# Gated attention with a mixture of experts on one core: zero products at the start, the first x tiles on two queues, an earlier weight copy, and another form and order for a few score tiles

## The chip, the core and the metric

The kernel runs on one core of a Trainium2 chip. The core has a matmul engine (PE, with weight loads shown as PEld), a vector engine (DVE), a scalar engine (ACT), GpSimd (POOL) and SyncE (SP), each with an instruction stream of its own that runs in order, and 16 DMA engines that move data between the main memory and the core's own memory. DMAs are issued here by SP, ACT and POOL. The metric is the device time of one execution in microseconds.

## The reference

x has 2 batches of 2048 rows of 512 numbers. Cut to what matters:

```
xn  = layernorm(x)
a   = layernorm(xn) * gamma + beta           # the attention's own norm
q, k, v = a @ Wq, a @ Wk, a @ Wv
out = softmax(causal(q k^T / sqrt(512))) @ v @ Wo + xn
f   = sum over the 2 best of 8 experts of gate * (silu(xn @ W1[e] + b1[e]) @ W2[e] + b2[e])
y   = x + out * silu(f)
```

## The kernel before

**Stages.** All matmuls are in float32, and the trace shows two records for each of them. (1) Wq and Wk are folded into one 512 x 512 matrix `wqk`, and Wv and Wo into `wvo` (`fold`, L207). Each fold goes over four row blocks c of its two sources; for every block it needs that block of both. (2) Eight blocks of 512 rows are normalised (`norm`), transposed into keys, and multiplied with `wqk` and `wvo`; for five of them by seven half-size products in place of eight (`seven_products`, L400). (3) `route` picks two experts for each row and sorts the rows. (4) The experts work through 68 steps of 128 rows (`up` L882, `down` L921). In the last of them a tile holds 64 rows for each of two experts; the second expert's weights are copied into `w1c` by ACT and into `w2c` by DVE (`copy_w2`, L869). The PE runs the two 64-wide streams side by side. (5) Attention goes over 32 query tiles of 128 rows in the order `seq` (L811), as pairs.

**How the work is ordered.** The whole order is written by hand: under `tc.manual_schedule()` every engine gets its instructions in program order. A step `s` of the attention's loop issues the scores of tile `seq[s]`, the softmax of the same tile, and the product with v of an earlier tile. `widths[s]` are the chunks of 512 keys of a tile, the last one cut at the diagonal.

**The start.** `load_raw(c, (0, 1))` issues row block c of the first source on SP and of the second on ACT. After c = 1, `load(0)` issues the four tiles of the first x block, all on SP (L160). Then follow the rest of the row blocks, `load(1)`, eight small loads, and the sources of the second fold: `parts[2]` on SP, `parts[3]` (o_proj) on ACT. The second fold follows the transposes of block 0 (L286). `gw` is a tile that DVE sets to zero at the start (L165) and that gets the router's weights later.

**The end of the experts.** `experts_step(i)` (L934 and following) issues for step i: the copy of w2c for tile i - 3, the output copy of tile i - 4, the join of the transposed halves for tile i - 2, and `down` of tile i - 3. After the last full step, the scores of tile 0 of the attention (`chunk_scores`, L994, maxima L982) are issued, and then the last expert steps.

**Scores by seven products.** For a pair in `FAST` (L959), the first 1024 keys of both tiles are scored together by `fast_scores` (L1046): 7 products of two half-depth matmuls, and sums of them on DVE (L1052). It needs sums of the queries (`query_sums`, L1013 to L1016) and of the first two key blocks (`block_sums`, L1027). The first product is copied to the score tile by ACT (L1065). A pair outside `FAST` is scored tile by tile (`chunk_scores`) and its exponentials (L1138) read the matmul's result directly. `FAST` also sets whether the products with v of a pair go by seven products (`combine_p`, `combine_v` L1210, L1236) or straight (`values`, L1188).

**Softmax to values.** The exponentials go to POOL, which splits the 16-bit halves (L1148), by a transposing DMA (L1154) and to DVE, which joins the halves (`join_p`, L1170). Tiles with at most 384 keys are transposed by PE (`turn_p`, L1165). `gather_y` (L1333) fetches the experts' rows and `gate` (L1343 to L1346) scales them; `attended` (L1351, L1354) and `emit` finish a tile.

**The second batch.** Its pairs come in the order 8-9, 0-1, 6-7, 2-3, 4-5, 10-11, 12-13, 14-15; the last three are in `FAST`. The table `later` (L1401) names the steps at whose end DVE prepares differences of the second batch's v blocks and key blocks, one instruction at a time.

Of the kernel before, what the change touches and what calls it, by code (L numbers as in the profile page):

```python
# [10 lines left out]
F32 = mybir.dt.float32  # L11
# [9 lines left out]
P = 128  # L21
# [5 lines left out]
def gated_attention_moe(  # L27
# [27 lines left out]
    nc = tc.nc  # L55
    B, S, D = x.shape
    E, _, H = w1_t.shape
    KEY = o_proj.shape[0]
    NT = B * S // P
    BT = 4  # L60
    TB = BT * P
    NB = NT // BT
    NBB = S // TB
# [9 lines left out]
    NS = -(-((2 * NT * P + E * (HALF - 1)) // HALF) // 2)  # L73
# [83 lines left out]
    def load(b):  # L157
        xt = xp.tile([P, BT, D], F32, name=f"x_{b}", tag="x")
        for t in range(BT):
            nc.sync.dma_start(out=xt[:, t, :], in_=xb[:, b * BT + t, :])  # L160
        xin[b] = xt

    GW = P // ND
# [540 lines left out]
        put(LAST - 5 + e, load_w1, e)  # L704

    in_order = ctx.enter_context(tc.manual_schedule())
    for c in range(NK):
        load_raw(c, (0, 1))
        if c == 1:
            load(0)  # L710
# [97 lines left out]

    assert B == 2 and NBB == 4
    seq = [t for t in reversed(range(NBB * BT))]  # L810
    seq += [NBB * BT + t for t in (8, 9, 0, 1, 6, 7, 2, 3, 4, 5, 10, 11, 12, 13, 14, 15)]  # L811
    assert all(seq[s] // 2 == seq[s + 1] // 2 for s in range(0, NT, 2))
    fetch_k = fetch(aks, lambda: kp2, kt_d, "k2", "kT")
    fetch_v = fetch(avs, lambda: vp, v_d, "v2", "v")
# [5 lines left out]
    DOWN = 3  # L820
# [44 lines left out]
    def copy_w2(i):  # L865
        if i >= FULL:
            ev = expert(places(i)[1][1], mybir.EngineType.DVE)
            for rows, c in ((P, slice(0, NH - 1)), (HL + 1, slice(NH - 1, NH))):
                nc.vector.tensor_copy(  # L869
                    w2c[:rows, c, :],  # L870
                    w2[:rows, bass.ds(ev, 1), c, :].rearrange("p o c d -> p (o c) d"),
                )
# [61 lines left out]
    def experts_step(i):  # L934


        def at(f, k):
            if 0 <= i + k < NS:
                f(i + k)

        at(copy_w2, -DOWN)
        at(keep_y, -DOWN - 1)
        if i >= 0:
            at(gather, FIRST)
        at(turn, 3)
        at(join, 1)
        at(join_h, -2)
        at(up, 0)
        at(turn_h, 0)
        at(copy_w1, 1)  # L950
        at(down, -DOWN)
# [5 lines left out]


    FAST = (0, 1, 2, 3, 13, 14, 15)  # L959

    def place(s):
        b, t = divmod(seq[s], BT)
# [21 lines left out]

    def direct(s):

        return range(2 if s // 2 in FAST else 0, len(widths[s]))

    def chunk_scores(s, j):
        b, t, first = place(s)  # L990
# [16 lines left out]
    def query_sums(s, engine):  # L1007

        q = qsums[s] = sq.tile([P, 4, ND // 2, P], F32, name=f"sq_{s}", tag="sq")
        (a11, a12), (a21, a22) = (  # L1010
            [aqs[seq[s] // 2][:, d, ts(seq[s + i] % 2, P)] for d in kds] for i in range(2)
        )
        engine.tensor_tensor(q[:, 0], a21, a22, ALU.add)  # L1013
        engine.tensor_tensor(q[:, 1], q[:, 0], a11, ALU.subtract)
        engine.tensor_tensor(q[:, 2], a11, a21, ALU.subtract)
        engine.tensor_tensor(q[:, 3], a12, q[:, 1], ALU.subtract)  # L1016
# [90 lines left out]
    for i in range(NS):  # L1107
        experts_step(i)
        if i >= 8 and i % 2 == 0 and early:
            f, b, c = early.pop(0)  # L1110
            f(b, c)
            if not early:
                query_sums(0, nc.gpsimd)
    for s in range(2):
        begin_scores(s)
    for j in direct(0):
# [277 lines left out]
    K = NBB  # L1394
# [5 lines left out]

    later = {}  # L1401
    for steps, f, b in (
        ((10, 10, 11, 11), combine_v, K + 2), ((12, 12, 13, 13), combine_v, K + 1),
        ((20, 21, 22, 23), block_sums, K), ((24, 25, 26, 27), combine_v, K),
    ):
        for i, step in enumerate(steps):
            later.setdefault(step, []).append((f, b, (i + 1,)))
# [6 lines left out]

    for s in range(NT + OUT + 2):
        fast = s // 2 - 1 in FAST
        pair = (s, s + 1) if s // 2 in FAST else (s,)
        if s < NT and (s % 2 == 0 or len(pair) == 1):
            for k in pair:
                if s:  # L1420
                    begin_scores(k)
                room(k)
        n = s // 2 + 1
        if s % 2 == 0 and NQ <= n < NT // 2:
            for c in range(2):
                fetch_q(n, c)
        if s == 0:
            fetch_parts(s, NBB * ND)
            block_sums(0)
        late = []  # L1430
        for k in range(NT):
            if k not in AHEAD:
                wait = 4 - k % 2 if k // 2 in FAST else 3
                if s == k + wait:
                    late.append((attended, k))
                if s == k + wait + 1:
                    emit(k)
        if len(pair) == 1 or s % 2:
            for f, *args in late:
                f(*args)  # L1440
        for k in range(NT):
            if s == (NT - 1 if k in AHEAD else k + 2 - k % 2 if k // 2 in FAST else k + 1):
                fetch_inputs(k)
        if s == NT - 1:
            gather_y(NT - 2)
        if s % 2 and s > 3 and s // 2 + 1 in FAST:
            query_sums(s + 1, nc.vector)
        joins = []
        for k in () if s == 1 else (0, 1) if s == 2 else (s - 1,):
            if 0 <= k < NT - 1 and not by_te(k):  # L1450
                joins += [(join_p, k)] * len(halves[k])
        chunks = []
        if s < NT and s != 1:
            chunks = [(k, j) for k in ((1,) if s == 0 else (s,)) for j in direct(k)]
        if s == 0:

            for k, j in chunks:
                chunk_scores(k, j)
            chunks = []
        if s < NT and s % 2 == 0 and len(pair) == 2:  # L1460
            pools = [(ps_a, "a")] * 5 + [(ps_b, "b"), (ps_a, "a")]
            if s < 3:
                pools = [(ps_b, "b")] * 3 + [(ps_a, "a")]
            if s == 2:
                joins = [(combine_v, b, (1,)) for b in range(NBB - 1)] + joins
            now = 5 if s == 2 else 1
            fast_scores(s, pools, late + joins[:now])
            joins = joins[now:]
            if s == 0:
                query_sums(2, nc.gpsimd)  # L1470
        for k, j in chunks:
            chunk_scores(k, j)
            if s != 3 and joins:
                f, *args = joins.pop(0)
                f(*args)
        if s != 3:
            for f, *args in joins:
                f(*args)
        if 0 <= s - 1 < NT and by_te(s - 1):

            values(s - 2)
            turn_p(s - 1)
        if s < NT and s != 1:
            end_scores(s)
        if fast and s % 2 == 0 and 2 < s < NT:
            combine_p(s - 2)
        if 0 <= s - 1 < NT:
            divisor(s - 1)
        if s < NT:
            if s != 1:  # L1490
                exponentials(s)
            if s % 2 == 0 and len(pair) == 2:
                maximum(s + 1, turned[s + 1][:, : 2 * TB], 0)
            if s == 0:
                end_scores(1)
                exponentials(1)
            fetch_parts(s, 4)
            for f, *args in later.pop(s, []):
                f(*args)
        if s == 2:  # L1500
            pass
        elif s == 3:
            combine_p(0, (1, 3, 2))
            for b in range(NBB - 1):
                combine_v(b, (2,))
            values_first(0)
            combine_p(0, (4,))
            for b in range(NBB - 1):
                combine_v(b, (4,))
            values_next(0)  # L1510
            for f, *args in joins:
                f(*args)
            values_end(0, [lambda: query_sums(s + 1, nc.vector)])
        elif fast and s % 2 == 0:
            values_first(s - 2)

            if s != NT - 2:
                values_next(s - 2)
        elif fast and s == NT - 1:
            values_next(s - 3)  # L1520
            gate(s - 1)
            values_end(
                s - 3, [lambda: join_p(s)] * len(halves[s]) + [lambda: combine_p(s - 1)]
            )
            for k in AHEAD:
                make_ahead(k)
        elif fast:
            values_end(s - 3)
        elif 0 <= s - 2 < NT and not (s - 1 < NT and by_te(s - 1)):
            values(s - 2)  # L1530

        for k in range(0, NT - 2, 2):
            if s == (k + 2 if k + 2 in AHEAD else k + 3):
                gate(k)
        for k in range(0, NT - 2, 2):
            if s == k + 1:
                gather_y(k)
        if s == 1:
            for b in range(NBB - 1):
                combine_v(b, (3,), nc.gpsimd)  # L1540
    att.close()

# [43 lines left out]
```

## Time and profile before

| | us |
|---|---|
| median of 3 runs | 1054.38 (1052.28 to 1054.64) |
| the profiled execution | 1051.26 |
| its span on the core | 1049.5 |
| PE busy | 1036.8 (99%) |
| DVE busy | 633.6 (60%) |
| POOL busy | 435.1 (41%) |
| ACT busy | 332.2 (32%) |
| first matmul | 3.93 |
| start of the attention's first scores | 592.65 |
| start of the second batch's first scores | 819.45 |

How to read it: the span begins with the first instruction and ends with the last, and the execution's own time is a little longer. A row of the timeline has the start, the length, the engine, the line, the operation, out<-in by the program's names, the shape, the number of merged instructions and in brackets the idle time before and what ended it. A row of the waits has the engine and line that waited, what it waited for, and total us, times and the longest. A row of the chain has start, length, engine, name and line, and the number of records. The columns of the DMA view are equal slices of the window that was asked for (here 0 to 24 us, 40 slices of 0.6 us).

### The profile page before, as it was taken

The numbers are of one execution on the slowest core, as the hardware profiler recorded it, in microseconds if no ns is written. First come the engines' busy times: TensorE is split into PE (matmuls) and PEld (weight loads), VectorE is DVE, ScalarE is ACT, GpSimd is POOL, SyncE is SP. The second block draws the span as 40 slices with busy tenths as digits, with TensorE's granted clock in tenths as the row PEclk, the third lists the DMA queues.
The fourth block names the chain that finished last, engine by engine and source line by source line (L and its number), as shares of the span: only waits on it lengthen the run. The fifth ranks groups of instructions, "written<-read, shape, count | busy, mean of one in ns | idle before, by whom it ended". The sixth has DMA issues, their size and how long they took to land.

```text
span 1049.5 us, 12196 instructions
## 1 busy us (share of the span) xinstructions
PE 1036.8 (99%) x3554; PEld 616.1 (59%) x3554; DVE 633.6 (60%) x1195; ACT 332.2 (32%) x675; POOL 435.1 (41%) x469
## 2 busy tenths in 40 slices
PE   8999999999999999999999999999999999999998
PEld 3688886444555555555545445776765544447577
DVE  4798884775333333333335468796656556789686
ACT  3222311211332232232246313213334554532340
POOL 2364250003433333335332117444656777764272
PEclk9999999999999999999999999999999999999999
DMA  8699999946999999999887256534767868754361
GB/s 304 180 283 288 296 240 329 344 163 172 195 238 225 225 218 240 224 230 229 198 189 165 64 197 163 143 91 123 192 175 223 269 188 229 184 139 126 96 158 41
DMA packets 300513, 209.34 MB, mean 199 GB/s; under 512 B 234520, under 2 KB 247576, under 8 KB 299424
## 3 DMA queue, kind: packets, MB, share of 16 engines
q1 hardware_dynamic: 281248, 146.12, 56.7%
q0 software_dynamic: 10560, 35.17, 13.3%
q10 hardware_dynamic: 8640, 27.27, 7.1%
q8 instruction: 30, 0.49, 0.2%
q14 instruction: 35, 0.29, 0.1%
HBM read 92.89 MB, written 60.03 MB: 146 GB/s over the span
## 4 chain that ended last, share of the span: by engine, by line
PE 84%; DMA 5%; DVE 3%; issue 3%; POOL 2%; ACT 1%; SPq 1%; ACTq 0%; DVEq 0%; POOLq 0%
PE py L921 16%; PE ph L882 16%; PE ps L994 13%; PE p L1236 9%; PE p L1046 8%; PE po L1188 7%; PE p L400 7%; DMA w<-in_w_t_dram 2%; PE p L1188 2%; PE pj L341 2%; PE pw L207 2%; PE pj L346 1%; DMA zuT<-zu 1%; ACT w1c L863 1%; POOL xs L768 1%
## 5 line engine op out<-in xcount | busy, mean ns | idle before, releaser
L921 PE MATMUL py<-w,ht 128*128 (+3 forms) x408 | 187.1, 594 | 0.0
L882 PE MATMUL ph<-w,xT 128*128 (+1 forms) x544 | 173.1, 460 | 0.7 <-POOL keep L1103 0.7
L929 DVE COPY y<-py 128x512 f32<-128x512 f32 x68 | 46.9, 690 | 174.1 <-PE py L921 170.5
L907 ACT ACTIVATE ht<-ht,b1sel 128x128 f32<-128x128 f32 (+3 forms) x237 | 73.1, 375 | 224.0 <-DVE ht L901 224.0
L994 PE MATMUL ps<-k,q 128*128 128x512 f32 (+3 forms) x416 | 143.0, 495 | 0.0
L882 PEld LDWEIGHTS ph<-w,xT 128*128 128x128 f32 (+1 forms) x544 | 97.4, 181 | 73.4 <-issue 34.5
L892 POOL COPY hu<-h 128x704 uint16<-128x704 uint16 x68 | 52.7, 775 | 203.6 <-ACT h L890 114.1
L1148 POOL COPY pu<-pT 128x1024 uint16<-128x1024 uint16 (+2 forms) x74 | 82.0, 1139 | 116.7 <-issue 53.1
L921 PEld LDWEIGHTS py<-w,ht 128*128 128x128 f32 (+3 forms) x408 | 73.4, 182 | 75.5 <-issue 38.4
L994 PEld LDWEIGHTS ps<-k,q 128*128 128x128 f32 x416 | 74.6, 190 | 67.6 <-issue 58.6
L768 POOL DMA_INDIRECT xs<-zu_d,toki x68 | 69.0, 1014 | 70.1 <-DVE toki L642 58.8
L1333 POOL DMA_INDIRECT yg<-y_d,posi x64 | 68.2, 1065 | 38.3 <-DVE yg L1344 22.8
L1188 PE MATMUL po<-v,pT 128*128 128x512 f32 x182 | 81.0, 592 | 0.0
L264 POOL COPY zu<-z 128x1024 uint16<-128x1024 uint16 x32 | 35.2, 1099 | 78.2 <-DVE z L249 78.2
L1170 DVE COPY pT<-puT 128x1024 uint16<-128x1024 uint16 (+2 forms) x74 | 54.9, 772 | 7.4 <-DMA puT<-pu 4.7
L1188 PEld LDWEIGHTS po<-v,pT 128*128 128x128 f32 x182 | 34.2, 190 | 38.1 <-issue 36.4
L413 DVE TENSOR_TENSOR so<-p,so 128x512 f32<-128x512 f32 x70 | 45.8, 686 | 15.2 <-DMA v_d<-so 9.0
L842 DVE COPY xT<-xhT 128x1024 uint16<-128x1024 uint16 x68 | 47.1, 692 | 11.0 <-DMA xhT<-xs 6.0
L1138 ACT ACTIVATE pT<-pT,nm 128x1024 f32<-128x1024 f32 x14 | 16.1, 1149 | 110.3 <-DVE nm L1082 71.3
L1138 ACT ACTIVATE pT<-ps,nm 128x512 f32<-128x512 f32 (+3 forms) x52 | 30.0, 580 | 61.0 <-DVE nm L1082 38.9
L1354 DVE SCALAR_TENSOR_TENSOR o<-xo,xscale,o 128x512 f32<-128x512 f32 x30 | 28.8, 965 | 33.3 <-ACT o L1351 32.0
L1052 DVE TENSOR_TENSOR pT<-p,pT 128x512 f32<-128x512 f32 x49 | 32.9, 687 | 25.9 <-PE p L1046 18.7
(246 smaller groups left out, 1705.7 us busy)
## 6 DMA issues: line engine op xcount, KB each, us to landing
y_d<-y SPq DMA_DIRECT2D x68, 256.0 KB
zu_d<-zu SPq DMA_DIRECT2D x32, 264.0 KB
x<-in_x_dram SPq DMA_DIRECT2D x32, 256.0 KB
kt_d<-kT ACTq DMA_DIRECT2D x8, 1024.0 KB
k<-kt_d SPq DMA_DIRECT2D x32, 256.0 KB
q<-qt_d SPq DMA_DIRECT2D x32, 256.0 KB
v<-v_d SPq DMA_DIRECT2D x32, 256.0 KB
xo<-in_x_dram SPq DMA_DIRECT2D x32, 256.0 KB
```

The lines of the kernel that those rows point to most:

```text
L400: nc.tensor.matmul(ps[:, r, :], lhsT=lhs[:, c, ts(r, P)], rhs=rhs[:, c, :], start=(c == 0), stop=(c == 1),)
L768: nc.gpsimd.indirect_dma_start(out=xs, out_offset=None, in_=zu_d, in_offset=bass.IndirectOffsetOnAxis(ap=toki[:, i : i + 1], axis=0),)
L882: nc.tensor.matmul(ph[at, :], lhsT=xT[:, c, at], rhs=rhs[k], start=(c == 0), stop=(c == ND - 1),)
L907: nc.scalar.activation(ht[:hn, c, at], ht[:hn, c, at], AF.Silu, bias=b1sel[:hn, c, j : j + 1])
L921: nc.tensor.matmul(py[at, :], lhsT=ht[:k, c, at], rhs=rhs[n], start=(c == 0), stop=(c == NH - 1),)
L994: nc.tensor.matmul(ps[:, :w], lhsT=aqs[seq[s] // 2][:, c, ts(t % 2, P)], rhs=aks[first + j][:, c, :w], start=(c == 0), stop=(c == ND - 1),)
L1046: nc.tensor.matmul(ps, lhsT=x[:, c], rhs=y[:, c], start=(c == 0), stop=(c == ND // 2 - 1))
L1148: nc.gpsimd.tensor_copy(pu[:, : 2 * w].rearrange("p (h d) -> p h d", h=2), turned[s][:, k : k + w].bitcast(U16).rearrange("p (d h) -> p h ...
L1170: nc.vector.tensor_copy(turned[s][:, k : k + w].bitcast(U16).rearrange("p (i t h) -> p i t h", t=P, h=2), puT[:, : 2 * w // P, :].rearrang ...
L1188: nc.tensor.matmul(dst, lhsT=turned[s][:, ts(k, P)], rhs=avs[first + k // BT][:, k % BT, cols], start=(start and k == k0), stop=(k == k1 - 1),
L1236: nc.tensor.matmul(dst, lhsT=a[:, k], rhs=v(k), start=(k == 0), stop=(stop and k == n - 1))
L1333: nc.gpsimd.indirect_dma_start(out=y, out_offset=None, in_=y_d, in_offset=bass.IndirectOffsetOnAxis(ap=posi[k][:, n : n + 1], axis=0),)
```

## The change

It has six parts. (a) Six products of zeros (`gw` with itself, 128 x 128) are issued on PE ahead of everything else. (b) The second and fourth tile of the first x block are issued on ACT's queue, the others stay on SP's. (c) The copy of w2c for the first expert tile after the last full step is issued ahead of the attention's first scores; in `experts_step(NS)` it is left out. (d) The second batch's first pair (steps 16 and 17, tiles 8 and 9) is scored by `fast_scores`; its product with v stays as it was. Its key sums are prepared at the ends of steps 13 to 15, and v differences of block K + 1 move from steps 12 and 13 to 20 to 23. At step 17 the joins of tile 8's halves are issued behind the exponentials of tile 9. (e) The pair 6-7 comes ahead of the pair 0-1. (f) Three POOL instructions at step 1 are issued for the blocks 2, 0, 1 in place of 0, 1, 2.

```diff
     def load(b):
...
-            nc.sync.dma_start(out=xt[:, t, :], in_=xb[:, b * BT + t, :])
+            queue = nc.scalar if b == 0 and t % 2 else nc.sync
+            queue.dma_start(out=xt[:, t, :], in_=xb[:, b * BT + t, :])
...
     in_order = ctx.enter_context(tc.manual_schedule())
+    warm = ps_t.tile([P, TB], F32, name="warm", tag="pt")
+    zeros = gw.rearrange("p c e -> p (c e)")
+    for _ in range(6):
+        nc.tensor.matmul(warm[:, :P], lhsT=zeros, rhs=zeros, start=True, stop=True)
     for c in range(NK):
         load_raw(c, (0, 1))
...
-    seq += [NBB * BT + t for t in (8, 9, 0, 1, 6, 7, 2, 3, 4, 5, 10, 11, 12, 13, 14, 15)]
+    seq += [NBB * BT + t for t in (8, 9, 6, 7, 0, 1, 2, 3, 4, 5, 10, 11, 12, 13, 14, 15)]
...
-        at(copy_w2, -DOWN)
+        if i != NS:
+            at(copy_w2, -DOWN)
...
     FAST = (0, 1, 2, 3, 13, 14, 15)
+    SCORED = FAST + (8,)
...
-        return range(2 if s // 2 in FAST else 0, len(widths[s]))
+        return range(2 if s // 2 in SCORED else 0, len(widths[s]))
...
+    copy_w2(NS - DOWN)
     for s in range(2):
         begin_scores(s)
...
-        ((10, 10, 11, 11), combine_v, K + 2), ((12, 12, 13, 13), combine_v, K + 1),
-        ((20, 21, 22, 23), block_sums, K), ((24, 25, 26, 27), combine_v, K),
+        ((10, 10, 11, 11), combine_v, K + 2), ((13, 14, 14, 15), block_sums, K),
+        ((20, 21, 22, 23), combine_v, K + 1), ((24, 25, 26, 27), combine_v, K),
...
-        pair = (s, s + 1) if s // 2 in FAST else (s,)
+        pair = (s, s + 1) if s // 2 in SCORED else (s,)
...
-        if s % 2 and s > 3 and s // 2 + 1 in FAST:
+        if s % 2 and s > 3 and s // 2 + 1 in SCORED:
             query_sums(s + 1, nc.vector)
...
+        behind = []
+        if s % 2 and s // 2 in SCORED and s // 2 not in FAST:
+            behind, joins = joins, []
...
                 exponentials(s)
+            for f, *args in behind:
+                f(*args)
...
-            for b in range(NBB - 1):
+            for b in (2, 0, 1):
                 combine_v(b, (3,), nc.gpsimd)
```

## The prediction

> **What bounds the kernel now.** I read the page's first part, then the waits of the matmul engine, then the timelines where the diff acts.
>
> ```profile
> PE 1036.8 (99%) x3554; PEld 616.1 (59%) x3554; DVE 633.6 (60%) x1195; ACT 332.2 (32%) x675; POOL 435.1 (41%) x469
> ```
> ```profile
> PE pw L207 <- DMA w<-in_qkv_t_dram: 4.1, 2, 3.9
> PE py L921 <- DVE w2c L869: 0.9, 1, 0.9
> PE p L1236 <- DVE u L1253: 0.8, 1, 0.8
> ```
>
> PE is busy for 1036.8 of 1049.5 us; its waits that have a releaser sum to 7.9 us. So a saving is either matmul time taken out or one of these waits shortened, and anything else counts only if it makes PE wait. Three places remain: the start, the end of the experts (about 600 us) and the first pair of the second batch (819 to 838 us). The timeline of the start:
>
> ```profile
> 3.93 8.93 PE L207 MATMUL pw<-w,w 128*128 128x512 f32 x16 [3.93 <-DMA w<-in_qkv_t_dram]
> 5.80 0.34 PEld L207 LDWEIGHTS pw<-w,w 128*128 128x128 f32 x1 [0.52 <-issue]
> 6.65 0.34 PEld L207 LDWEIGHTS pw<-w,w 128*128 128x128 f32 x1 [0.52 <-issue]
> 10.53 0.69 DVE L234 BATCH_NORM_STATS2 st<-x 128x6 f32<-128x512 f32 x1 [0.45 <-DMA x<-in_x_dram]
> 13.07 7.10 PE L207 MATMUL pw<-w,w 128*128 128x512 f32 x16 [0.21 <-DMA w<-in_qkv_t_dram]
> 17.22 1.85 SPq L201 DMA_DIRECT2D w<-in_qkv_t_dram  x4
> 22.32 13.90 PE L207 MATMUL pw<-w,w 128*128 128x512 f32 x32
> ```
>
> Weight loads 0.85 us apart (5.80, 6.65) mean records at half pace; the last 16 records take 7.10 us, 0.43 each. At 13.07 PE waits for the third row block of weights.
>
> **Start: zeros and two queues.** Full pace would put 16 records from 3.93 at 3.93 + 6.87 = 10.80, and 16 more at 17.67; the first fold really ends at 20.01. So at most 2.3 us can go: 1.9 of half pace (the first 16 took until 12.7: 12.86 less the last record's drain of 0.16) and 0.4 of waiting until 13.07. Neither edit does it alone: without an earlier third block, faster records only wait longer, and without faster records the block saves 0.4.
>
> *Queues.* On SP the third block lies behind four x tiles, whose landings the statistics show (they start at 7.76, 9.18, 10.53, 11.76). With two of these on ACT's queue it should take the third x tile's place, about 10.5 us. ACT's own third block is now fifth on its queue, as SP's is, so I take the same time for it. All four o_proj loads move behind, and ACT issues the last near 11 us, ahead of the first square root (12.98 now); I expect the root at 12.6 (load issue, then the 1.28 us table load) and z by 16.6, where the transposes want it from 18.3. If this cover is gone, each us costs one. The windows' DMA column reads 388 GB/s from 5 to 10 us already, so no bytes come sooner in total; only the order changes.
>
> [...]
>
> *Zeros.* Six products are 12 records of 128 columns. Transposes of that width run 0.11 us apart at full pace, so 0.22 at half: 2.6 us. They can begin after the memset of gw (0.91 + 0.17), so they end about 3.9: free, or up to 0.2 late. The half pace lasted 3.6 us from the first matmul (3.93 to about 7.5), though the profile's granted clock reads 1.00 there, so that column does not show it. If the count begins with the zeros, full pace comes at 4.9 to 5.2; the first fold then loses 0.5 to 0.7 of the 1.9 us and ends at about 18.3. If it doesn't, all 1.9 stay. I take the first, as the only ramp in the trace started with PE work.
>
> [...]
>
> *What is late next.* The second fold follows 2.31 us after the first (transposes, 20.01 to 22.32): 20.6. Its weights are the four SP loads issued at 17.22 behind the small loads, which the change doesn't move. The DMA view by slices of 0.6 us:
>
> ```profile
> GB/s 0 0 0 89 297 399 408 405 410 365 369 362 410 396 396 396 389 403 382 389 386 389 386 393 393 389 174 20 2 5 28 60 147 399 396 393 406 401 405 405
> ```
>
> The queue is nearly empty from 15.6 to 19.2 and fast from 19.8 on, so the first 256 KB are in at about 20.6 to 20.8. The fold starts at 20.8: **1.5 us** (0.4 with no earlier full pace, 2.2 if the weights come sooner too). It reaches the end as PE stays dense; DVE work behind it is released by PE (the add at 41.38) and moves along.
>
> **End of the experts: weights copied sooner.** Timeline at 600 us:
>
> ```profile
> 599.64 1.07 PE L921 MATMUL py<-w,ht 128*64 x2
> 600.15 0.69 DVE L982 TENSOR_REDUCE mx<-ps 128x1 f32<-128x512 f32 x1
> 600.76 1.02 DVE L869 COPY w2c<-w 128x1024 f32 x2
> 601.59 0.61 PE L921 MATMUL py<-w2c,ht 128*64 128x512 f32 x1 [0.88 <-DVE w2c L869]
> ```
>
> Two half-width streams, w and w2c, run side by side. The copy for the w2c stream sits on DVE behind the scores' maxima, which wait for PE. Moved ahead of the scores it runs at about 592 to 593 (PE's last use of w2c ends near 592.6), when DVE idles 7 us. Both streams then start at 599.64 and end at 599.64 + 6 x 0.43 = 602.2. The next tile is then gated by its own steps: maximum until 600.84, y copy 0.69, join 0.55, first Silus 0.3, so PE at 602.4, its w2c copy (0.69) at 602.8, against 604.37 now; the last tile ends at 608.05 against 609.5. **1.45 us**; bounds 0.9 (only the idle shown) and 1.95 (601.59 less 599.64). No DMA is moved.
>
> **First pair of the second batch.** From the chain, in matmul records:
>
> ```profile
> 819.45 7.76 PE ps L994 x24
> 829.04 8.60 PE ps L994 x24
> 838.49 0.89 PE ps L994 x8
> 847.11 1.73 PE ps L994 x8
> 907.92 12.02 PE p L1046 x28
> ```
>
> Now: 7.76 + 8.60 = 16.36. After: 12.02 for seven products, 0.89 and 1.73 for the two diagonal chunks = 14.64. PE saves 1.72. DVE adds seven adds (0.69 each) and two wide maxima (1.22), drops four maxima (0.69): +4.5 us, and the query sums (four of about 0.42) before tile 15's maximum. The block sums (four of 1.22) move from steps 20-23 to 13-15, where DVE has idle 2.2 and 2.5 us stretches behind ACT; their keys are issued at 806.88, wanted at 809.7, so I expect at most a few tenths. K+1's v differences move the other way, unneeded before step 28. On SP the query, input and output DMAs of the swapped pairs trade places, their number unchanged. The POOL order 2, 0, 1 starts when all v have landed (645.11): nothing.
>
> Does tile 16's softmax come in time? ACT copies the first product behind the gate of pair 12, about 827.5 (exponential of tile 15 later by the 1.7 us of query sums). Six adds, a maximum, the last add and the diagonal chunk bring DVE to 835.5; ACT exponentiates at 836 (after its table load), POOL copies at 837.2. Now POOL starts at 831.50 and the first join at 835.94, 4.45 later; so 841.7, done by 842.4. PE reaches these values after 819.45 + 12.02 + 0.89 + 1.72 + 0.11 + 1.73 + 0.86 + 6.01 = 842.8. That 6.01 is the score of tile 6, moved ahead of the short tiles; with a short one (0.89) PE would stall some 5 us. Slack 0.4, error of the row sums 1 to 3 us: stall 0 to 2.8, taken 0.4. **1.3 us** (1.7 to minus 1.1). The short tiles at steps 20-22 have 6 us from score to transpose at the least, against 7.2 for the same kind at 812.0 to 819.23, unstalled: nothing.
>
> **Sum.** 1.5 + 1.45 + 1.3 = 4.25 us. The profiled execution took 1051.26 (span 1049.5, 1.76 around it): 1047.0. It lies 3.1 under the median 1054.38 of the runs, which spread over 2.4; the same saving from the median gives 1050.1, my forecast. About 0.3%, 3.2 us, is what can be told from no change.
>
> **Rivals.** (1) The half pace stays, or the third block doesn't come sooner: the start gives 0 to 0.45, sum 2.75 to 3.2, 1051.2 to 1051.6. For it: one ramp is no law. Against: both conditions have rows. (2) Tile 16's joins come 2.8 late: the pair costs 1.1 net, sum 1.85, 1052.5. For it: slack of 0.4 behind three in-order engines. Against: I counted the queues full. (3) Slower: ACT's copy of the first product is held in its queue by pair 12's gate, waiting for gathered rows. DVE's adds, then the joins, wait for it; beyond 0.4 us of lateness PE pays one for one. It ends slower by 0.3% if the copy comes 7.8 us late (about 835): 1057.6. Against: ACT takes these rows at 821.67 without a wait.
>
> **Numbers.** Forecast 0.70 (gain 3.2 to 5.8: 1048.6 to 1051.2), rival 1 0.13, rival 2 0.12, rival 3 0.05. Faster 0.70, same 0.25 (rivals 1 and 2), slower 0.05. The range takes in rivals 1 and 2 and, at the low end, 1.2 us of the runs' spread: 1047.4 to 1053.0.
>
> **What shows it.** Weight loads 0.43 apart from about 5 us and no wait at the third block; second fold at 20.8; w2c stream beginning with w at the experts' end; 28 records L1046 at the pair and no PE wait on L1170 after it. A second fold still near 22, or PE idle before tile 16's values, would make it wrong.

## The result and the profile after

| | before | after |
|---|---|---|
| median | 1053.66 us (13 runs) | 1059.1 us (13 runs) |
| lowest to highest | 1051.87 to 1054.64 | 1055.63 to 1064.45 |
| ratio, 95% interval | | 1.0054 (1.0041 to 1.0067) |
| profiled execution | 1051.26, span 1049.5 | 1059.1, span 1057.4 |
| mean granted TensorE clock of that execution | 1.000 | 0.996 |

The kernel became slower by 0.5%; the prediction, 1050.1 and probably faster, was wrong. Line numbers below are those of the changed kernel: the products stand at L1055, the block sums at L1036, the query sums at L1022 to L1025, values at L1198, joins at L1180. First the first part of its page and the waits of the matmul engine (us in total, times, longest):

```profile
PE 1039.6 (98%) x3562; PEld 617.2 (58%) x3562; DVE 645.7 (61%) x1204; ACT 332.2 (31%) x672; POOL 435.5 (41%) x469
```
```profile
PE p L1055 <- DVE sq L1023: 2.9, 1, 2.9
PE pg L309 <- DVE zT L292: 2.8, 1, 2.8
PE po L1198 <- DVE pT L1180: 2.3, 1, 2.3
...
PE p L1055 <- ACT pT L1148: 1.0, 1, 1.0
...
PE pw L209 <- DMA w<-in_qkv_t_dram: 0.2, 1, 0.2
```

The waits for the third block of weights (0.2 in before) and for w2c (0.9) are gone, as meant; the wait for the first weights (3.9 in before) is now mostly filled with zeros, and the first fold starts at 4.16 in place of 3.93. Four new or longer waits stand in the list, 9.0 us in all (the one for L292 was 0.5 in before). And PE's busy time rose by 2.8 us. The zeros are 2.9 of it; but 1.72 of products and up to 1.9 of half pace at the start should have come off, so 1.6 to 3.5 us of matmul time are new.

**Start.** Timeline, then transfer rates of the first 24 us in slices of 0.6 us:

```profile
1.13 2.93 PE L713 MATMUL warm<-gw 128*128 128x128 f32 x12 [1.13 <-DVE b1s L169]
...
4.16 14.27 PE L209 MATMUL pw<-w,w 128*128 128x512 f32 x32
...
20.97 3.27 PE L209 MATMUL pw<-w,w 128*128 128x512 f32 x7 [0.23 <-DMA w<-in_qkv_t_dram]
```
```profile
GB/s 0 0 0 37 195 391 406 392 420 393 331 399 399 389 399 396 389 386 393 369 393 393 382 386 396 382 315 57 6 3 31 47 87 362 399 314 413 401 401 405
```

The first fold is one group of 32 records with no wait. The second begins at 20.97 in place of 22.32 and waits for its weights, as the prediction said. The rates are about those of before (peaks of 420 and 410 GB/s); what changed is the order. But at block 3 (fourth router product, L307 in before, L309 now) PE is late. First the row of before, then that of the changed kernel:

```profile
89.94 1.06 PE L307 MATMUL pg<-zT,gw 128*32 128x512 f32 x8 [0.47 <-DVE zT L290]
...
91.03 1.07 PE L309 MATMUL pg<-zT,gw 128*32 128x512 f32 x8 [2.81 <-DVE zT L292]
```

The attention's first scores start at 592.66 against 592.58. So in this execution the whole gain of the start is lost by then, in the wait of 2.8 us.

**End of the experts.** The two streams now begin together, as predicted:

```profile
599.73 0.64 PE L928 MATMUL py<-w,ht 128*64 x1
599.73 0.64 PE L928 MATMUL py<-w2c,ht 128*64 128x512 f32 x1
```

From the first scores to the last w2c product this stage is 1.7 us shorter (592.58 to 608.89 before, 592.66 to 607.26 after).

**The pair.** From 816 to 916 us PE goes from 1.3 us ahead of before to 7.8 behind. The timeline of the place:

```profile
810.48 1.23 DVE L1036 TENSOR_TENSOR tk<-k,k 128x1024 f32<-128x1024 f32 x1 [2.31 <-DMA k<-kt_d]
...
816.61 2.18 DVE L1036 TENSOR_TENSOR tk<-k,tk 128x1024 f32<-128x1024 f32 x1
...
818.71 2.28 DVE L1036 TENSOR_TENSOR tk<-k 128x1024 f32<-128x1024 f32 x1
...
819.87 2.25 POOL L1372 TENSOR_TENSOR o<-o,yg 128x512 f32<-128x512 f32 x1
...
820.92 1.75 DVE L1364 SCALAR_TENSOR_TENSOR o<-xo,xscale,o 128x512 f32<-128x512 f32 x1
...
822.59 1.48 DVE L1022 TENSOR_TENSOR sq<-q 128x256 f32<-128x256 f32 x1
824.10 0.42 DVE L1023 TENSOR_TENSOR sq<-sq,q 128x256 f32<-128x256 f32 x1
...
824.58 8.47 PE L1055 MATMUL p<-tk,sq 128*128 128x512 f32 x12 [2.87 <-DVE sq L1023]
```

The block sums first wait 2.31 us for their keys. Then DVE is solid up to the query sums, and while POOL works on `emit`'s sums (L1372, L1373) the same instructions take longer: 2.18 and 2.28 in place of 1.23, 1.48 in place of 0.42. PE has made the two products that need no query sum and waits 2.87. (The bracket and the waits view count from the modelled end of the last record, 0.59 us after its start, while records of 512 columns in a row lie 0.43 apart; taken from record to record, each wait is 0.16 longer.) The next view is by windows of 5 us (busy us and count of PE, PEld, DVE, ACT, POOL; then the granted clock, DMA share, GB/s):

```profile
815.00:820.00 5.00, 4.81 (x14) 2.34 (x14) 4.90 (x8) 3.05 (x6) 4.59 (x5) 1.00 0.49 147
820.00:825.00 5.00, 2.13 (x5) 0.83 (x5) 4.97 (x6) 0.00 (x0) 4.69 (x3) 0.89 0.74 236
825.00:830.00 5.00, 5.00 (x7) 1.90 (x7) 3.54 (x9) 4.02 (x7) 1.44 (x2) 0.50 0.97 338
830.00:835.00 5.00, 5.00 (x12) 2.13 (x11) 3.89 (x6) 1.16 (x3) 4.21 (x4) 0.92 0.58 164
```

DVE is busy 4.90 and 4.97 of 5 us, PE 2.13. And the clock is 0.50 from 823.93 to 830.75, 6.83 us. Its first 0.65 us fall into the wait; from 824.58 on records lie 0.85 us apart in place of 0.43. So the wait costs its 2.9 us and, behind it, 3.1 of matmul time (half of the 6.17 from 824.58 to 830.75). That is the new matmul time of the first part.

The other new wait stands at the short tiles that now come last:

```profile
897.76 1.86 SPq L801 DMA_DIRECT2D v<-v_d  x4
...
901.35 1.35 SPq L1164 DMA_TRANSPOSE puT<-pu  x1
...
909.93 0.70 DVE L1180 COPY pT<-puT 128x1024 uint16<-128x1024 uint16 x1 [4.26 <-DMA puT<-pu]
...
910.78 3.67 PE L1198 MATMUL po<-v,pT 128*128 128x512 f32 x8 [2.32 <-DVE pT L1180]
```

Tile 3's transpose is issued 3.6 us behind four loads of v, and the join that waits for it starts 8.6 us after its issue. In before:

```profile
887.59 1.87 SPq L794 DMA_DIRECT2D v<-v_d  x4
...
894.80 1.23 SPq L1154 DMA_TRANSPOSE puT<-pu  x1
...
899.23 0.82 DVE L1170 COPY pT<-puT 128x1024 uint16<-128x1024 uint16 x1
```

There the transpose came 7.2 us behind the loads, and the join began 4.4 us after it, without a wait and 5.1 us ahead of need.

**The sum** between 816 and 924 us: waits of 2.87, 0.43 (before tile 16's values), 2.32 and 1.04 are 7.3 from record to record; half clock 3.1; less 1.72 of products saved: 8.7, against 9.1 seen.

### The profile page after: what moved, and what is told of

Read it like the earlier page. It is cut to its first block, busy times and chain, and to the rows that moved or that the text cites. A ratio compares the mean times of both kernels' runs of the same rounds, so it can differ in the third digit from the quotient of the medians.

```text
span 1057.4 us, 12223 instructions
## 1 busy us (share of the span) xinstructions
PE 1039.6 (98%) x3562; PEld 617.2 (58%) x3562; DVE 645.7 (61%) x1204; ACT 332.2 (31%) x672; POOL 435.5 (41%) x469
## 4 chain that ended last, share of the span: by engine, by line
PE 69%; DMA 9%; issue 7%; POOL 7%; DVE 5%; SPq 2%; ACT 2%; ACTq 0%; POOLq 0%; DVEq 0%
PE py L928 16%; PE ph L889 15%; PE p L1246 9%; PE ps L1003 8%; PE p L1055 7%; PE p L402 3%; PE po L1198 3%; DMA w<-in_w_t_dram 2%; PE p L1198 2%; PE pj L343 2%; DMA zuT<-zu 2%; PE pw L209 1%; PE pj L348 1%; DMA w<-in_qkv_t_dram 1%; POOL o L1372 1%
## 5 line engine op out<-in xcount | busy, mean ns | idle before, releaser
L1003 PE MATMUL ps<-k,q 128*128 128x512 f32 (+3 forms) x384 | 129.3, 487 | 0.0
L1003 PEld LDWEIGHTS ps<-k,q 128*128 128x128 f32 x384 | 68.6, 190 | 60.4 <-issue 50.7
L1198 PE MATMUL po<-v,pT 128*128 128x512 f32 x182 | 81.3, 594 | 2.9 <-DVE pT L1180 2.3
L1180 DVE COPY pT<-puT 128x1024 uint16<-128x1024 uint16 (+2 forms) x74 | 57.1, 803 | 9.1 <-DMA puT<-pu 9.1
L1198 PEld LDWEIGHTS po<-v,pT 128*128 128x128 f32 x182 | 34.0, 190 | 41.9 <-issue 39.3
L1061 DVE TENSOR_TENSOR pT<-p,pT 128x512 f32<-128x512 f32 x56 | 37.5, 686 | 28.4 <-PE p L1055 19.3
L1148 ACT ACTIVATE pT<-pT,nm 128x1024 f32<-128x1024 f32 x16 | 18.4, 1149 | 113.0 <-DVE nm L1091 73.8
L1055 PE MATMUL p<-tk,sq 128*128 128x512 f32 x96 | 45.9, 629 | 3.9 <-DVE sq L1023 2.9
L1372 POOL TENSOR_TENSOR o<-o,yg 128x512 f32<-128x512 f32 x30 | 43.1, 1437 | 12.8 <-DVE o L1364 12.6
```

The source lines that it names most:

```text
L1003: nc.tensor.matmul(ps[:, :w], lhsT=aqs[seq[s] // 2][:, c, ts(t % 2, P)], rhs=aks[first + j][:, c, :w], start=(c == 0), stop=(c == ND - 1),)
L1055: nc.tensor.matmul(ps, lhsT=x[:, c], rhs=y[:, c], start=(c == 0), stop=(c == ND // 2 - 1))
L1180: nc.vector.tensor_copy(turned[s][:, k : k + w].bitcast(U16).rearrange("p (i t h) -> p i t h", t=P, h=2), puT[:, : 2 * w // P, :].rearrang ...
L1198: nc.tensor.matmul(dst, lhsT=turned[s][:, ts(k, P)], rhs=avs[first + k // BT][:, k % BT, cols], start=(start and k == k0), stop=(k == k1 - 1),
L1372: nc.gpsimd.tensor_tensor(o, o, g, ALU.mult)
```

## The experiments

Each kernel was measured against before in the same series; medians and ratios to before.

**1. Without the pair's parts** (scores of tile 8 and 9 direct, old order, old `later`; start, copy and POOL's order stay).

```diff
-    SCORED = FAST + (8,)
+    SCORED = FAST
-    seq += [... (8, 9, 6, 7, 0, 1, 2, 3, ...)]
+    seq += [... (8, 9, 0, 1, 6, 7, 2, 3, ...)]
-        ((13, 14, 14, 15), block_sums, K), ((20, 21, 22, 23), combine_v, K + 1),
+        ((12, 12, 13, 13), combine_v, K + 1), ((20, 21, 22, 23), block_sums, K),
```

> The change without its parts (d) and (e): no seven products for the second batch's first pair, old order of the short tiles, old steps for the key sums and v differences; zeros, two queues, early weight copy and POOL order stay. Theory: the pair is where the time went (in the changed kernel's trace PE waits 2.9 us for the query sums at 821, runs 6.8 us at half clock, and waits 2.3 and 1.0 us near 908 and 920), so without it 1052.3 us (1053.7 less the 1.4 that PE is ahead at 816 us), clock 1.000, and PE's wait for L1023's tile is gone. Rival, that the start or the copy costs time somewhere: 1055 or more.

Measured: 1051.27, 0.9976 (0.9964 to 0.9988). The pair's waits are gone; the one at block 3 remains (2.8, and 3.41 us of half clock behind it).

**2. The pair's parts alone** (before with (d) and (e)).

> The kernel before plus parts (d) and (e) alone. Theory: 1060.5 us (1053.7 plus the 5.4 of the medians and the 1.4 that the other parts bring), half clock for some us right after a wait for the query sums. Rival, that the pair's trouble comes from its neighbours being early: at most 1056.

Measured: 1060.57, 1.0061 (1.0039 to 1.0082). The same two waits, and the clock falls behind both, here in windows:

```profile
825.00:830.00 5.00, 2.14 (x5) 0.73 (x4) 4.95 (x7) 0.00 (x0) 4.28 (x3) 0.87 0.82 253
...
910.00:915.00 5.00, 1.42 (x7) 0.91 (x5) 0.60 (x1) 0.00 (x0) 2.65 (x3) 0.90 1.09 202
915.00:920.00 5.00, 4.76 (x6) 2.19 (x7) 3.88 (x9) 1.80 (x5) 3.22 (x4) 0.50 0.84 275
```

The rival fell. Both kernels together: the pair's parts are the loss, some 7 to 8 us, and what is left is a gain of 2.5.

**3. The start's parts alone** (before with (a) and (b)).

> The kernel before plus zeros and two queues alone. Theory: PE is 1.3 us ahead at the second fold and loses all of it at 90 us, where the chain goes through a transposing DMA (wait 2.8 us in the changed kernel's trace): 1053.7, within 0.6 either way. Rival, that what was won at the start stays: 1052.3.

Measured: 1052.45, 0.9992 (0.9979 to 1.0006): closer to the rival, but not to be told from no change, nor from half of the 1.5 us. No run has the copy (c) or POOL's order (f) alone. From this kernel to kernel 1, which adds both, the ratio falls by 0.16%, or 1.7 us, but the intervals overlap.

**4. PE kept busy in the stall.** The second product of pair 8 is made three times (3.4 us of repeats that write the same values) so that PE does not idle while DVE is late.

```diff
         p2 = made(a12, b21)
+        if s == 2 * 8:
+            for _ in range(2):
+                for c in range(ND // 2):
+                    nc.tensor.matmul(p2, lhsT=a12[:, c], rhs=b21[:, c], start=(c == 0), stop=(c == ND // 2 - 1))
```

> The changed kernel; the second of the seven products at step 16 is made three times over (the two repeats write the same values), so that PE works 3.4 us in place of waiting 2.9 us for the query sums. Theory, that the half clock after the wait costs 3.4 us of its own: 1056.2 us, clock 1.000 in the pair, and the runs lie closer together than 1055.6 to 1064.5. Rival, that the wait alone is the loss and the clock doesn't matter: 1059.6.

Measured: 1057.5, 1.0044 (1.0027 to 1.0062). In the pair the clock stays at 1.00 in every window from 815 to 840, and the runs lie closer (1056.4 to 1060.3, though these are 6 and those were 13). DVE is as busy as before (4.90 and 4.95 of 5 us). POOL works 4.90 and 4.27 of 5 (4.59 and 4.69 in the changed kernel). So here the half clock came with PE's idling, not with DVE's or POOL's work. That the repeats also cost less than the wait is not shown: the interval overlaps that of the changed kernel. The wait for tile 3's join (2.7) stayed, with 3.41 us of half clock.

**5. Sums earlier**: keys fetched at step 11, block sums at steps 12 to 14, query sums at step 15 ahead of the finishing work.

```diff
-               (12, fetch_k, K), (14, fetch_v, K), ...
+               (11, fetch_k, K), (14, fetch_v, K), ...
-        ((13, 14, 14, 15), block_sums, K),
+        ((12, 13, 13, 14), block_sums, K),
+        if s == 15:
+            query_sums(s + 1, nc.vector)
```

> The changed kernel with block K's keys fetched one step earlier (11), its key sums at the ends of steps 12, 13, 13, 14, and the query sums at step 15 ahead of the attended tile on DVE. Theory, that the first loss is DVE's lateness with these sums (wait 2.9 us, then 3.4 us of half clock): the wait for the query sums is gone, 1053 us (1059.1 less 6), the wait near 908 stays. Rival, that the seven products' later chain (adds, softmax, joins of tile 16) is as late as the sums and only takes over: above 1057, with a new PE wait on the joins near 840.

Measured: 1055.88, 1.0021 (1.0007 to 1.0035), between theory and rival. The wait for the sums is gone and so is the half clock there. The sums still take their long times beside POOL (2.18 for the last key sum, 1.37 to 1.49 for three of the query sums); they only begin sooner. Keys, key sums and query sums were moved together, so the share of each is not shown. New: 1.7 us before tile 16's values at 840, and the wait for tile 3's join grew to 4.2, again with 3.41 us of half clock.

**6. v loads later**: `fetch_v` of block K + 3 from step 22 to 25.

> The changed kernel with the last v block's four loads moved from step 22 to step 25. Theory, that tile 3's transposes (issued at 901, landed at 910) come late behind these loads on SP's queue: PE's wait near 908 (2.3 us) and the one at 919 (1.0) go, and with them the half clock that this wait set off in other runs: 1055.5 us. Rival, that the short tiles' order alone leaves too little cover, loads or not: the wait stays above 1.5 us, 1058.5 or more.

Measured: 1056.41, 1.0033 (1.0016 to 1.005). The wait for tile 3's join is gone: its transpose is issued at 901.67 and the join begins at 905.91. So the v loads ahead of the transpose on SP were its cause; whether by their place in SP's queue or by the engines that both share is not shown. The other waits stay, the one at 919 too (1.2), against the theory.

**7. Both 5 and 6.**

> Both edits of the two kernels before it. Theory, that these two waits and their half clock are all that the pair costs: 1049.6 us, the 1051.3 of the kernel without the pair less the 1.72 of matmul records that seven products take out, clock 1.000 from 100 us on; faster than the kernel before by 0.4%. Rival, that something else of the pair (DVE's 4.5 us more, the narrower cover of tile 16) costs as much as it saves: 1051.3 or more.

Measured: 1053.31, 0.9999 (0.9983 to 1.0014). The gains add up (0.33% and 0.21% apart, 0.55% together), yet it misses the 1049.6: 1.7 us before tile 16's values and 1.2 for ACT's exponential (L1148) near 914 remain, together more than the 1.72 that seven products save. That is a net 1.2 of the 0.23% (2.4 us) between this kernel and kernel 1; what the rest is, the trace does not show.

**8. The order alone**: the changed kernel without the products (`SCORED = FAST`, old `later`), with 6-7 ahead of 0-1.

> The changed kernel without the seven products (old steps for the sums), but with the pair 6-7 ahead of 0-1. Theory, that the second loss belongs to the order of the short tiles: PE waits 2 to 4 us for tile 3's join before the first late pair (about 900 us here), 1054.5 us. Rival, that it comes from the products' DVE work: no such wait, 1051.3 as without the pair.

Measured: 1055.52, 1.0021 (1.0004 to 1.0039), 0.45% over kernel 1, which differs by the order alone. Its rows:

```profile
896.49 1.23 SPq L1164 DMA_TRANSPOSE puT<-pu  x1
...
904.52 0.95 DVE L1180 COPY pT<-puT 128x1024 uint16<-128x1024 uint16 x1 [3.70 <-DMA puT<-pu]
...
905.61 4.61 PE L1198 MATMUL po<-v,pT 128*128 128x512 f32 x5 [3.09 <-DVE pT L1180]
```

and 6.83 us of half clock from 904.85 on, of which 6.1 behind the wait: 3.1 + 3.0 in this execution. The theory held.

**9. x loads later**, on kernel 1, for the wait at block 3: `load(b + 2)` put three places further on.

```diff
-                put(at - STEP + 4, load, b + 2)
+                put(at + 1, load, b + 2)
```

> The kernel without the pair's parts, with the x loads of blocks 4 to 7 issued three units later in the projections (behind the keys of the block that frees their place). Theory, that PE's wait for block 3's transposed rows at 88 to 92 us (0.6 to 3.7 us in ten profiles) comes from x loads that share the DMA engines with the last transposing DMA: the wait falls below 1 us, no half clock at 91, and the runs give 1049.5. Rival, that the transposing DMA is late by its own queue: wait and time as without this edit, 1051.3.

Measured: 1050.18, 0.9965 (0.995 to 0.998). It tells nothing of the cause: SP issued these loads at 84.06 all the same (84.67 in kernel 1), and the wait stayed (2.9). The loads' issue on SP ends at 88.56 and its next one stands at 94.39, so SP was not short of time; a place further on in the program moved no load. The time is in effect a second measurement of kernel 1.

**10. First product copied by DVE** in place of ACT, on kernel 7.

> The kernel with both mends, and at step 16 the first product is copied by DVE in place of ACT, whose copy stands behind pair 12's gate until 830.6 while DVE waits 2.0 us for it. Theory, that this queue is what makes PE wait 1.9 us before tile 16's values (844): that wait falls below 0.5, 1051.6. Rival, that the wait follows from the transposing DMAs and joins alone: wait and time unchanged, 1053.3.

Measured: 1052.48, 0.9995 (0.9977 to 1.0014). The wait before tile 16's values fell from 1.7 only to 1.0, and the time is not to be told from kernel 7's.

**11. Old order on kernel 10.**

> The kernel before this one in the list (both mends and DVE's copy) with the old order, pair 0-1 ahead of 6-7. Theory, that the order is needed by the seven products: with a short score tile as cover PE waits some 5 us for tile 16's joins and then runs at half clock (3.4), against 1.4 us saved near 916: 1058. Rival, that the order costs more than it covers: at most 1051.6.

Measured: 1057.82, 1.0044 (1.0024 to 1.0065), as the theory said.

```profile
840.65 9.67 PE L1198 MATMUL po<-v,pT 128*128 128x512 f32 x17 [6.02 <-ACT yg L1353]
```

The releaser named, the gate on ACT (839.66, 1.32 long), ends only after PE's start; tile 16's joins begin at 839.00 on DVE and are the likelier one. The products need the new order as cover, and the new order itself costs (kernel 8, with the v loads in their old place; with later v loads and without the products it was not run).

**12. Row stores behind the transposes**, on kernel 1, for the wait at block 3.

```diff
-            nc.sync.dma_start(out=zu_rows[:, b * BT + t, :], in_=zu)
+        for t in range(BT):
+            nc.sync.dma_start(out=zu_rows[:, b * BT + t, :], in_=zus[t])
```

> The kernel without the pair's parts, and on SP the four row stores zu_d of each block are issued behind the block's four transposes in place of between them. Block 3's last transpose was issued at 81.41 in the kernel without the pair, 10.9 us after the first, with three row stores (1.45, 1.59, 1.84 us) between. Theory (the waiting of PE near 88 is the end of this chain of issues, which takes 19 to 21.5 us from POOL's first copy whatever PE does): the last transpose is issued about 4 us sooner, PE's wait on L309 falls from 2.96 to under 1, no half clock follows, and the time falls to 1047.5 to 1049.5. Rival (the transposes' own landing, 7.4 to 9.2 us behind the last issue, paces the chain, or the v stores that hold DVE at L415 do): the wait stays above 2, 1050.2 to 1051.5, or worse if the stores reach the next block's rows.

Measured: 1055.25, 1.0029 (1.0014 to 1.0045); its profiled execution was the fastest of 12, at 1051.4.

```profile
71.81 10.99 SPq L273 DMA_TRANSPOSE zuT<-zu  x4
...
86.60 0.69 DVE L416 TENSOR_TENSOR so<-p,so 128x512 f32<-128x512 f32 x1 [2.69 <-DMA v_d<-so]
...
87.21 2.49 DVE L293 COPY zT<-zuT 128x1024 uint16<-128x1024 uint16 x4
```

The same place in kernel 1:

```profile
70.47 1.25 SPq L273 DMA_TRANSPOSE zuT<-zu  x1
...
81.41 1.92 SPq L273 DMA_TRANSPOSE zuT<-zu  x1
...
87.30 0.69 DVE L415 TENSOR_TENSOR so<-p,so 128x512 f32<-128x512 f32 x1 [4.74 <-DMA v_d<-so]
...
90.56 0.69 DVE L292 COPY zT<-zuT 128x1024 uint16<-128x1024 uint16 x1 [0.77 <-DMA zuT<-zu]
```

My theory fell. Without the stores between them the last transpose is issued 8.8 us after the first (at 80.62), in place of 10.9: half of the 4 us that I expected, because one of the transposes alone now takes 4.1 us to issue. In both kernels the joins stand on DVE behind a sum that waits for the store of v (2.69 here, 4.74 in kernel 1). The wait of PE fell from 2.96 to 1.5, taken from record to record, but two like it appear at later blocks (1.4 at 150 us, 1.6 at 170), and the runs became slower. Why its other runs are up to 8.6 us longer no trace shows.

## Why the prediction was wrong

Nearly every sign that I had named came true (weight loads 0.43 apart from 5 us, no wait at the third block, second fold at 20.97, both w2c streams together, 28 records of the pair, only 0.43 of idling before tile 16's values), and yet the kernel is slower: no sign looked at the query sums.

**Start, forecast 1.5.** Right in this execution: second fold at 20.97 (20.8 forecast). Over all traces it begins at 20.7 to 21.8 with the edits and at 22.3 and 22.8 without. That full pace comes a fixed time after the zeros begin was wrong: I forecast 4.9 to 5.2, and it comes at 4.7 to 7.1 (last section), so 4.73 here was partly luck. "It reaches the end as PE stays dense" failed: at block 3 PE waits 0.5 in before, but 2.4 in the pair alone and up to 3.5 with the start's edits, and what arrives there comes through a transposing DMA (9.50 us in the chain, from 80.75 to 90.25 in the changed kernel), not from PE. What is left is about 1 us (kernel 1's 2.5 less the copy's 1.7), too little to measure alone. What sets that wait stays open: kernel 9 moved nothing, and kernel 12's shorter wait lies within the spread of the other traces with the start's edits (1.2 to 3.7 us from record to record).

**Copy, forecast 1.45.** Right: 1.7 in the trace, bound 1.95, though no run has it alone. With what the start leaves, kernel 1 gains 2.5.

**Pair, forecast 1.3 faster; measured some 7 slower.** The step that failed is the one on DVE: block sums at steps 13 to 15 "at most a few tenths", and "the query sums (four of about 0.42)". I checked only whether the sums had room, by their durations alone, and not by when the last of them is done, with the finishing sum of an earlier tile (L1364) between them and the query sums. Keys came 2.31 late for DVE, and beside POOL's sums four instructions took about 1 us more each. The trace of before had such a row: the same finishing sum takes 0.75 at 814.57 and 1.64 at 818.91, where POOL is at `emit`.

```profile
814.57 0.75 DVE L1354 SCALAR_TENSOR_TENSOR o<-xo,xscale,o 128x512 f32<-128x512 f32 x1 [2.23 <-ACT o L1351]
...
818.91 1.64 DVE L1354 SCALAR_TENSOR_TENSOR o<-xo,xscale,o 128x512 f32<-128x512 f32 x1 [2.47 <-ACT o L1351]
```

Instead of tile 16's values, where I looked (0.43 of wait, 0.4 forecast), the query sums became late: 2.87, and 3.1 of half clock behind it.

**Order, forecast "nothing".** Failed: PE waits 2.3 to 4.2 us, by v loads on SP ahead of tile 3's transpose (kernels 6 and 8). I compared score-to-transpose times of tiles that PE transposes; tile 3 has 512 keys and goes by DMA (8.6 us from its issue to the join, 3.6 us behind the v loads).

**Missing altogether: the clock in the middle of the kernel.** Each wait was priced at one us for one us. Some waits of 2.9 us and more were followed by half clock that cost another 1.5 to 3.1. Rival 3 had the right side by another mechanism, and its chance, 0.05, was too small: a change that puts eight more sums on DVE ahead of a product deserved more. (Its sum takes the 0.4 of slack in twice: a copy 7.8 late gives 1057.1, not 1057.6.) "With a short one PE would stall some 5 us" was right (6.0 in kernel 11).

**What is best.** Kernel 1, the change without the pair's parts, beats both: 0.9976, and 0.9965 in its near copy, kernel 9.

## What to carry to other kernels

Price a moved instruction on an in-order engine by when it ends, with the durations it has beside its new neighbours (2.18 us beside POOL's sums here, 1.23 without), and follow it to the first matmul that needs it. A matmul wait can cost twice, once as idle time and once in the clock: 2.87 and 3.1 us for the query sums here, while the wait of 2.32 near 908 cost only itself. Look at what is issued ahead of a transposing DMA: 3.6 us behind four loads of v the join began 8.6 us after the transpose's issue, 7.2 us behind them 4.4, and with the loads moved later 4.2 (kernel 6).

## What the runs showed of the hardware

**The clock fell after some short waits of the matmul engine.** In the changed kernel's trace the first record of full clock is at 4.73 us; the granted clock is then 1.00 until 823.93, 0.50 until 830.75 and 1.00 again until 1056.03, behind the last matmul. The half clock begins 0.65 us before the wait of 2.87 ends. The stretches of half clock behind waits last 3.41 us (kernels 1, 4 and 5) or 6.83 (the changed kernel and kernel 8); the windows of kernel 2 give 3.4 and 6.8, those of kernel 11 give 6.8. The length of a wait alone does not decide: from record to record, waits of 2.90 (kernel 4) to 6.19 us (kernel 11) were followed by half clock, and so was one of 2.96 at block 3 in kernel 1. But in the changed kernel the one of 2.98 at the same block was not (the clock is 1.00 in every window from 84 to 96 us), nor was the one of 2.48 near 908 (1.00 in every window from 905 to 925). What decides between them is not shown; no run was made for it.

**The scatter of the runs goes with it.** The changed kernel's 13 runs follow their granted clock: 1055.6 at 0.998, 1059.3 on average at 0.995, 1064.5 at 0.992. The 29 runs of before in the series of kernels 9 to 11 do so too: 1051.7 on average at 1.000 (12 runs), 1054.9 at 0.998 (9). The lost clock itself is only part of it: 0.6% of 1060 us would be 6.4 of the 8.9 us, by estimate, and the 12 runs at 1.000 still lie between 1049.9 and 1053.2.

**With zeros at the start the full clock came sooner, by an amount that differs between executions.** PE's first record is at 1.13 us with zeros and at 3.9 without. The first record of full clock in the trace comes at 4.73 us in the changed kernel, at 4.7 to 7.1 in the twelve kernels with zeros, and at 7.57 (before) and 9.48 (kernel 2) in the two without. The pace agrees where both can be read: in before the records of the first fold are 0.85 us apart until 7.50 and 0.43 from 7.97 on, in the changed kernel 0.43 from 5.39 on. Why the twelve differ by 2.5 us is not shown.

**Sums of DVE and POOL took longer side by side.** In the changed kernel POOL's sum runs from 816.42 to 817.70 at its usual 1.28; DVE's of 1024, started at 816.61, ends at 818.79, 1.09 after it. POOL's next one, from 817.78, takes 2.14 and ends at 819.92; DVE's next, from 818.71, ends at 820.99, 1.07 after that. Both take about 2.2 us in place of 1.2 and 1.3: DVE's sum of the same size takes 1.23 at 810.48 and at 826.09, POOL's 1.28 at 831.98. The rows do not show what holds them up.
